# A hybrid attention kernel: the first Toeplitz blocks loaded during the attention, and one half's short lags taken in turns with the last chunks' norm and transform

## The chip, the cores and the metric

The kernel runs on one core of a Trainium2 chip. Its time is the device time of one execution in microseconds (us), taken over three runs; a profile of one further execution shows what each engine did. The engines are TensorE (PE in the profile, PEld for its weight loads), VectorE (DVE), ScalarE (ACT), GpSimd (POOL) and SyncE (SP), which here issues nearly all DMA transfers.

## The reference

Two batches of an image of 128 channels and 64 x 64 places go through a first layer (group norm, 7 x 7 neighbourhood attention, two small dense stages) and a second layer on 4096 tokens of 128 channels. The second layer is what the change touches:

```python
t = _to_tokens(x)
t = t + _L1_attn_ref(_ln_t(t))          # full attention of t with itself, diagonal masked
t = t + _L1_ffn_ref(_ln_t(t), ...)      # "ffn": a spectral unit, below

# in _L1_ffn_ref, for the branch that the gumbel argmax selects (T, T/2, T/4 or T/8 tokens):
U_plus, U_minus = _stu_conv(phi, u, PADDED_SL)        # causal convolution with 16 filters of length sl
out = einsum('btkd,k,kde->bte', U_plus, s, Mpp) + einsum('btkd,k,kde->bte', U_minus, s, Mpm)
for i in range(3):                                    # short lags: tokens t, t-1, t-2
    out = out + einsum('btd,de->bte', shifted(u, i), Mu[i])
```

## The kernel before

**Attention.** `attention(b, fill)` runs for batch 0, then batch 1. The tokens are eight chunks of 512. For each pair of chunks PE computes the products (L896), ACT exponentiates them (L903), PE turns them (L910), DVE copies the turned block and sums its rows (L913), and PE multiplies with the tokens (L924 into `own`, L949 into `other`). When a chunk is complete, `fill(c, part)` is told so; at every other step `fill()` is called without arguments and runs one piece of other work.

**Filler.** `filler(b, steps)` keeps a list `urgent` and the list `steps`. For a complete chunk it adds `after(b, c, part)` to `urgent`, and when four or eight chunks are complete also `short_lags(b, 0)` or `short_lags(b, 1)`. `fill()` runs the next piece of the first generator in `urgent`, or of `steps` if `urgent` is empty. For batch 1, `steps` holds what was left of batch 0 and `filter_matrices`, which loads the filters' matrices through two `st` buffers (L1102) and mixes them on DVE (L1105, L1107, L1118 to L1123). What is left when the attention ends is run then, one generator after another.

**Norm and transform of a chunk.** `after` turns the chunk (L973), divides and adds on DVE (L978), takes the layer norm (statistics L169 and L170 and L159 on DVE, the power on POOL at L160, the result z at L177 on DVE), turns z back (L188, copied to `zc` by ACT at L989), and multiplies it with a segment transform (L1009, L1017), whose results are copied (L1011, L1019) and stored to `us` in HBM (L998).

**Short lags.** `short_lags(b, h)` needs the four chunks of half h of the tokens. In eight pieces it turns the tokens (L188, copied to `xa` by ACT at L1032) and multiplies `zc` with the three matrices `mu` (L1041), which DVE adds to `xa` (L1048).

**Toeplitz products.** After the attention, `pair(q)` loads a block of the filters' transform (`ct`, four DMAs from `gs`, L1256) and a block of the segments' transform (`ut`, one DMA from `us`, L1258) into a pool `conv` of five buffers. `gs` is written during batch 0's attention. `group()` multiplies ct and ut (L1277) into a PSUM tile `pc`, and DVE and ACT copy that to `y` (L1278); `project` multiplies y with the filters' matrices (L1288). Four pairs are loaded ahead.

**What sets the order.** In the Toeplitz loop PE's order is that of the program text; elsewhere in this layer a scheduler orders each engine's instructions, so a DMA may stand earlier in SP's order than in the text. A tile waits for what last used its memory. The pool `conv` lies where `tok`, `cm` and other tiles of the attention lay, and is opened after the attention.

Of the kernel before, what the change touches and what calls it, by code (L numbers as in the profile page):

```python
# [8 lines left out]
F32 = mybir.dt.float32  # L9
# [5 lines left out]
P = 128  # L15
# [6 lines left out]
KF = 16  # L22
# [58 lines left out]
CB, FB, SG = 256, 8, 4  # L81
# [6 lines left out]
LG = 2 * FB  # L88
GROW = 4 * LG * KF
# [3 lines left out]
def kernel(  # L93
# [16 lines left out]
    nc = tc.nc  # L110
# [14 lines left out]
    for c in range(4):  # L125
# [19 lines left out]
        out=flip, in_=flip, compare_op=ALU.not_equal, fill=1.0, base=1 - QT * QT, pattern=[[0, 2], [1, QT * QT]],  # L145
# [39 lines left out]
    def transposed(ps, src):  # L185

        for j in range(src.shape[1]):
            nc.tensor.transpose(ps[:, j * P : (j + 1) * P], src[:, j, :], ident)  # L188
# [30 lines left out]
    with l0a:  # L219
# [34 lines left out]
        def table(ci, h, eng):  # L254
# [16 lines left out]
            out=gavg, in_=gavg, compare_op=ALU.is_ge, fill=0.0, base=0,  # L271
# [3 lines left out]
            out=gavg, in_=gavg, compare_op=ALU.is_ge, fill=0.0, base=3,  # L275
# [524 lines left out]
        for i in range(7):  # L800
# [53 lines left out]
    gs = dram.tile([BINS, 2, SG, GROW], F32, name="gs")  # L854

    with ap_:
# [6 lines left out]
        def bank():  # L863
            return ps_m.tile([P, 512], F32, tag="bank", name="bank")
# [159 lines left out]
        def short_lags(b, h):  # L1024


            for par in range(2):
                n0 = (par * 2 + h) * FB
                for f0 in range(0, FB, 4):
                    pt = bank()  # L1030
                    transposed(pt, tt[b][:, n0 + f0 : n0 + f0 + 4, :])
                    nc.scalar.copy(xa[b][:, (n0 + f0) * P : (n0 + f0 + 4) * P], pt)  # L1032
                    yield
                xv = xa[b][:, n0 * P : (n0 + FB) * P].rearrange("p (f c) -> p f c", f=FB)
                for c0 in range(0, P, 64):
                    py = bank()
                    for lag in range(3):
                        from_par = (par - lag) % 2
                        back = (lag - par + from_par) // 2
                        s0 = 1 + (h * P + c0) * FB - back  # L1040
                        nc.tensor.matmul(  # L1041
                            py, lhsT=mu[:, lag, :], rhs=zc[:, from_par, s0 : s0 + 512], start=(lag == 0), stop=(lag == 2)
                        )
                    pv = py.rearrange("p (c f) -> p f c", f=FB)
                    first = h == 0 and c0 == 0
                    for lo, hi, s in ((0, 32, 0), (32, 64, 1)) if first else ((0, 64, 2 + h),):
                        xs = xv[:, :, c0 + lo : c0 + hi]
                        nc.vector.scalar_tensor_tensor(  # L1048
                            xs, pv[:, :, lo:hi], seg[:, s : s + 1], xs, ALU.mult, ALU.add
                        )  # L1050
                    yield
# [57 lines left out]
        def filter_matrices(mpl, mmi):  # L1109

            for k0 in range(0, KF, 4):
                for dst, src in ((mpl, m_plus), (mmi, m_minus)):
                    mixed(dst[:, k0 : k0 + 4, :], src[:, k0 : k0 + 4])
                    yield

                a, d = (m[:, k0 : k0 + 4, :].rearrange("p k e -> p (k e)") for m in (mpl, mmi))
                s = sp.tile([P, 512], F32, tag="st", name="mdiff")
                nc.vector.tensor_tensor(s, a, d, ALU.subtract)  # L1118
                nc.vector.tensor_tensor(a, a, d, ALU.add)
                for k in range(4):  # L1120
                    ks = slice(k * P, (k + 1) * P)
                    nc.vector.tensor_scalar(a[:, ks], a[:, ks], sg[:, k0 + k : k0 + k + 1], None, ALU.mult)
                    nc.vector.tensor_scalar(d[:, ks], s[:, ks], sg[:, k0 + k : k0 + k + 1], None, ALU.mult)  # L1123
                yield
# [47 lines left out]
            yield from products(1, ((0, b0), (1, b1)))  # L1172
            yield from products(3, ((1, b0),))

        def filler(b, steps):

            urgent, done = [], []

            def fill(c=None, part=None):
                if c is not None:  # L1180
                    done.append(c)
                    urgent.append(after(b, c, part))
                    if len(done) % 4 == 0:
                        urgent.append(short_lags(b, len(done) // 4 - 1))
                    return
                for queue in (urgent, steps):
                    while queue:
                        if next(queue[0], 0) is None:
                            return
                        queue.pop(0)  # L1190

            return fill, urgent
# [25 lines left out]
        mpl = l1.tile([P, KF, P], F32, name="mpl")  # L1218
        mmi = l1.tile([P, KF, P], F32, name="mmi")
        inv = l1.tile([P, 3, CB], F32, name="inv")  # L1220
        steps = [*left, filter_matrices(mpl, mmi)]
        fill, left = filler(1, steps)
        attention(1, fill)
        for gen in (*left, *steps):
            for _ in gen:
                pass

# [8 lines left out]
        nc.vector.tensor_scalar(inv[:, :, lo:hi], inv[:, :, lo:hi], seg[:, s : s + 1], None, ALU.mult)  # L1236
    outf = out.rearrange("b c h w -> b c (h w)")
    with ExitStack() as cv:
        obp = cv.enter_context(tc.tile_pool(name="ob", bufs=1))
        cp = cv.enter_context(tc.tile_pool(name="conv", bufs=5))  # L1240
        ps_c = cv.enter_context(tc.tile_pool(name="ps_c", bufs=6, space=PSUM))
        ps_p = cv.enter_context(tc.tile_pool(name="ps_p", bufs=2, space=PSUM))

        ob = obp.tile([P, 2, NB, FB, BINS, 2], F32, name="ob")

        def pair(q):


            ct = cp.tile([P, 2, 320], F32, tag="ct", name="ct")
            for o in range(2):  # L1250
                for l in range(2):
                    src = bass.AP(
                        gs.tensor, gs.offset + 4 * q * SG * GROW + (2 * o + l) * LG * KF,
                        [[GROW, 4 * SG], [KF, FB], [1, (FB + l) * KF]],
                    )
                    nc.sync.dma_start(out=ct[:, o, l * 144 : l * 144 + (FB + l) * KF], in_=src)  # L1256
            ut = cp.tile([P, NB, 2, P], F32, tag="ut", name="ut")
            nc.sync.dma_start(  # L1258
                out=ut.rearrange("p b s d -> p (b s d)"),
                in_=us[2 * q : 2 * q + 2].rearrange("g i r f b s d -> (g i r f) (b s d)"),  # L1260
            )
            return ct, ut

        def group():


            y = cp.tile([P, 8, KF, 2, 32], F32, tag="y", name="y", bufs=2)
            for q in range(GB // 2):
                ct, ut = ahead.pop(0)
                for par in range(2):  # L1270

                    cv_ = ct[:, :, 0 : 288 + par * 32].rearrange("p o (l c) -> p o l c", l=2)[:, :, :, 0 : FB * KF]
                    for b in range(NB):
                        for f in range(2):
                            fp = slice(f * 64, (f + 1) * 64)
                            pc = ps_c.tile([P, 2, 2, FB * KF], F32, tag="pc", name="pc")
                            nc.tensor.matmul(pc, lhsT=ut[fp, b, par, :], rhs=cv_[fp], start=True, stop=True)  # L1277
                            (nc.scalar.copy if f else nc.vector.tensor_copy)(  # L1278
                                y[:, 4 * f : 4 * f + 4, :, par, b * 2 * FB + q : (b + 1) * 2 * FB : 2],
                                pc.rearrange("p r l (t k) -> p (r l) k t", k=KF),  # L1280
                            )
                if to_load:
                    ahead.append(pair(to_load.pop(0)))
            return y

        def project(g, y, acc, l, k):
# [42 lines left out]

        places = [(b, par, f0) for b in range(NB) for par in range(2) for f0 in range(0, FB, 2)]  # L1330
        to_load = list(range(BINS // 2))
        ahead = [pair(to_load.pop(0)) for _ in range(4)]
        rest = []
        with tc.manual_schedule(engines={mybir.EngineType.PE}):
            y = group()
# [128 lines left out]
```

## Time and profile before

| | |
|---|---|
| median of three runs | 2265.4 us (2261.26 to 2269.05) |
| profiled execution | 2264.99 us, span 2263.3 us, mean granted PE clock 0.988 |
| PE at 1260 to 1280 us, in batch 1's attention | busy 20.00 of 20 us |
| PE from 1307.3 to 1344.0 us, the end of the attention and what is left after it | busy 29.83 of 36.7 us |
| PE from 1344.0 to 1350.1 us | busy 0.01 of 6.1 us |
| PE at 1400 to 1420 us, in the Toeplitz loop | busy 20.00 of 20 us |
| all sixteen DMA engines over the span | 109.76 MB, 48 GB/s |

The busy time of an engine is the time in which it executes; idle time is put down to what ended it. The chain of waits follows the execution back from its last instruction, at each step to what released it. A row of PE's timeline counts records, and a 128 x 512 product in this precision has two.

### The profile page before, as it was taken

Reading aid. Unit: us, or ns where it says so; the run is one execution under the profiler, and the core shown is the slowest. Engines: PE = TensorE matmul, PEld = TensorE weight load, DVE = VectorE, ACT = ScalarE, POOL = GpSimd, SP = SyncE. Lnnn points to the kernel's source line nnn. Section 1 sums busy time; section 2 is a strip of 40 time slices with the busy share of each in tenths; the row PEclk is TensorE's granted clock in tenths of the full one; section 3 lists DMA queues with packets and bytes.
Section 4 is the critical chain, followed back from the end, with each engine's and each line's share of the span. In section 5 each row is a group of like instructions: output and inputs, shape, how many; then the busy total and the mean of one; then the engine's idle time right before and its main releaser. Section 6 shows DMA issues by size and latency. Waiting matters only on the chain.

```text
span 2263.3 us, 31741 instructions
## 1 busy us (share of the span) xinstructions
PE 2187.7 (97%) x11908; PEld 1354.1 (60%) x11908; DVE 940.2 (42%) x3047; ACT 785.3 (35%) x1911; POOL 277.3 (12%) x354
## 2 busy tenths in 40 slices
PE   5899998999999999999999979999999999999998
PEld 3677764544544444544544436777677777767777
DVE  4799985433444347433333333222213222232323
ACT  2789883222333223222222323223323222232322
POOL 3377874200000000000000000000000000000000
PEclk8999998999999999999999989999999999999999
DMA  4222213011100015100000133122222121222101
GB/s 119 63 62 61 61 50 50 0 52 56 38 24 19 6 52 155 33 24 23 1 24 24 39 87 92 42 55 58 44 53 58 39 58 39 57 45 52 41 8 75
DMA packets 180858, 109.76 MB, mean 48 GB/s; under 512 B 32225, under 2 KB 165857, under 8 KB 180194
## 3 DMA queue, kind: packets, MB, share of 16 engines
q1 hardware_dynamic: 177866, 105.47, 17.9%
q10 hardware_dynamic: 2840, 2.27, 0.4%
q8 instruction: 94, 1.54, 0.3%
q14 instruction: 58, 0.48, 0.1%
HBM read 73.09 MB, written 34.60 MB: 48 GB/s over the span
## 4 chain that ended last, share of the span: by engine, by line
PE 87%; DVE 5%; POOL 3%; DMA 1%; ACT 1%; issue 1%; SPq 1%; POOLq 0%; DVEq 0%; ACTq 0%
PE acc L1288 25%; PE pc L1277 13%; PE bank L896 10%; PE own L924 10%; PE other L949 8%; PE bank L910 4%; PE bank L331 2%; PE py L1315 2%; PE bank L188 2%; PE bank L1041 2%; PE bank L1009 2%; PE bank L541 1%; PE bank L1150 1%; PE po L563 1%; PE bank L505 1%
## 5 line engine op out<-in xcount | busy, mean ns | idle before, releaser
L1278 DVE COPY y<-pc 128x512 f32<-128x512 f32 x320 | 221.5, 692 | 358.9 <-PE pc L1277 355.2
L903 ACT ACTIVATE e<-bank 128x512 f32<-128x512 f32 x288 | 171.9, 597 | 563.1 <-PE bank L896 427.2
L896 PE MATMUL bank<-cm 128*128 128x512 f32 x576 | 298.4, 602 | 1.4 <-DVE y L652 1.4
L1277 PE MATMUL pc<-ct,ut 64*128 64x512 f32 x1280 | 287.4, 599 | 6.1 <-issue 6.1
L1288 PE MATMUL acc<-y,mpl 128*128 128x256 f32 x1280 | 292.1, 382 | 0.0
L1288 PE MATMUL acc<-y,mmi 128*128 128x256 f32 x1280 | 288.0, 379 | 0.0
L1288 PEld LDWEIGHTS acc<-y,mpl 128*128 128x128 f32 x1280 | 238.1, 190 | 59.4 <-issue 29.6
L1288 PEld LDWEIGHTS acc<-y,mmi 128*128 128x128 f32 x1280 | 242.6, 190 | 32.6
L1278 ACT COPY y<-pc 128x512 f32<-128x512 f32 x320 | 205.2, 641 | 93.7 <-PE pc L1277 93.7
L949 PE MATMUL other<-e,tok 128*128 128x512 f32 x448 | 228.6, 592 | 0.0
L924 PE MATMUL own<-et,tok 128*128 128x512 f32 x448 | 226.9, 593 | 0.7 <-DVE part L913 0.7
L913 DVE CUSTOM_DVE_ANT_0 et<-bank,one 128x512 f32<-128x512 f32 x224 | 145.7, 688 | 165.0 <-PE bank L910 164.9
L1277 PEld LDWEIGHTS pc<-ct,ut 64*128 64x128 f32 x1280 | 121.8, 188 | 152.8 <-issue 147.7
L1294 ACT COPY ob<-acc 128x256 f32<-128x256 f32 x40 | 24.1, 603 | 430.9 <-PE acc L1288 430.9
L924 PEld LDWEIGHTS own<-et,tok 128*128 128x128 f32 x448 | 84.6, 190 | 108.3 <-issue 72.6
L949 PEld LDWEIGHTS other<-e,tok 128*128 128x128 f32 x448 | 85.0, 190 | 106.6 <-issue 106.2
L896 PEld LDWEIGHTS bank<-cm 128*128 128x128 f32 x576 | 96.4, 193 | 72.4 <-issue 44.5
L1327 DVE TENSOR_TENSOR xa<-py,xa 128x512 f32<-128x512 f32 x32 | 22.2, 692 | 281.4 <-PE py L1315 281.4
L910 PEld LDWEIGHTS bank<-ident,e 128*128 128x128 f32 x896 | 103.3, 141 | 54.1 <-issue 46.2
L160 POOL TENSOR_TENSOR ln_rs<-ln_rs,mhalf 128x4 f32<-128x4 f32 x24 | 24.3, 1012 | 867.0 <-DVE ln_rs L159 867.0
L528 ACT ACTIVATE p<-p,mn 128x196 f32<-128x196 f32 x256 | 114.4, 449 | 22.0 <-DVE mn L518 14.0
L910 PE MATMUL bank<-ident,e 128*128 128x128 f32 x896 | 116.9, 273 | 0.0
(200 smaller groups left out, 2342.8 us busy)
## 6 DMA issues: line engine op xcount, KB each, us to landing
ut<-us SPq DMA_DIRECT2D x80, 256.0 KB
us<-ub SPq DMA_DIRECT2D x64, 256.0 KB
vw<-vd SPq DMA_DIRECT2D x256, 49.0 KB
ct<-gs SPq DMA_DIRECT2D x160, 72.0 KB
ct<-gs SPq DMA_DIRECT2D x160, 64.0 KB
gs<-ub SPq DMA_DIRECT2D x20, 256.0 KB
vd<-v SPq DMA_DIRECT2D x128, 32.0 KB
st<-in_m_plus_dram SPq DMA_DIRECT2D x16, 256.0 KB
```

The costliest lines, as they stand in the source:

```text
L188: nc.tensor.transpose(ps[:, j * P : (j + 1) * P], src[:, j, :], ident)
L331: nc.tensor.matmul(pl, lhsT=wg[:, lo : lo + P], rhs=zT, start=True, stop=True)
L528: nc.scalar.activation(p, p, AF.Exp, bias=t[name + "mn"][:, h : h + 1], scale=-1.0, accum_out=t["den"][:, u, h : h + 1],)
L896: nc.tensor.matmul(ps, lhsT=cm[b][:, n * P : (n + 1) * P], rhs=cm[b][:, chunk(c)], start=True, stop=True)
L903: nc.scalar.activation(e, ps, AF.Exp, bias=0.0, scale=ASCALE, accum_out=part[:, n, c : c + 1])
L910: nc.tensor.transpose(pt[:, k * P : (k + 1) * P], es[k][:, m * P : (m + 1) * P], ident)
L913: nc.vector.tensor_tensor_reduce(et, pt, one, 1.0, 0.0, ALU.mult, ALU.add, part[:, n, a : a + 1])
L924: nc.tensor.matmul(own, lhsT=tok[b][:, n, :], rhs=e, start=first, stop=last)
L949: nc.tensor.matmul(other, lhsT=tok[b][:, 4 * CHUNKS[a] + j, :], rhs=es[j], start=(j == 0), stop=(j == 3))
L1277: nc.tensor.matmul(pc, lhsT=ut[fp, b, par, :], rhs=cv_[fp], start=True, stop=True)
L1278: (nc.scalar.copy if f else nc.vector.tensor_copy)(y[:, 4 * f : 4 * f + 4, :, par, b * 2 * FB + q : (b + 1) * 2 * FB : 2], pc.rearrange("p ...
L1288: nc.tensor.matmul(acc, lhsT=(mmi if l else mpl)[:, k, :], rhs=y[:, 1::2, k, ::-1, :] if l else y[:, 0::2, k, :, :], start=(l == 0 and k = ...
```

## The change

It has four parts.

1. The tile `ct` moves out of `conv` into a pool `blocks` of its own, opened before batch 1's attention. `pair(q)` is split into `blocks(q)`, which loads ct, and `inputs(q)`, which loads ut.
2. A generator `load_blocks`, which loads ct for q = 0 to 3, is added to `steps` of batch 1 after `filter_matrices`. After the attention, only the four ut tiles are loaded ahead.
3. In batch 1, the short lags of the first half are put in a list `kept` instead of `urgent`. When the attention has ended, the rest of `steps` is run, and then what is left of `urgent` (the last chunks' `after` and the second half's short lags) in turns with the kept generator: one piece of the one, one piece of the other.
4. The pool `conv` is opened before the pool of `ob`, where it was opened after it.

```diff
-        def filler(b, steps):
+        def filler(b, steps, kept=None):
...
                     if len(done) % 4 == 0:
-                        urgent.append(short_lags(b, len(done) // 4 - 1))
+                        held = kept if kept is not None and len(done) == 4 else urgent
+                        held.append(short_lags(b, len(done) // 4 - 1))
...
-        steps = [*left, filter_matrices(mpl, mmi)]
-        fill, left = filler(1, steps)
-        attention(1, fill)
-        for gen in (*left, *steps):
-            for _ in gen:
-                pass
...
+        ctp = ctx.enter_context(tc.tile_pool(name="blocks", bufs=5))
+
+        def blocks(q):
+            ct = ctp.tile([P, 2, 320], F32, tag="ct", name="ct")
...
+            return ct
+
+        first_blocks = []
+
+        def load_blocks():
+            for q in range(4):
+                first_blocks.append(blocks(q))
+                yield
+
+        steps = [*left, filter_matrices(mpl, mmi), load_blocks()]
+
+        kept = []
+        fill, left = filler(1, steps, kept)
+        attention(1, fill)
+        for gen in steps:
+            for _ in gen:
+                pass
+        kept = kept.pop()
+        for gen in left:
+            for _ in gen:
+                next(kept, None)
+        for _ in kept:
+            pass
...
-        obp = cv.enter_context(tc.tile_pool(name="ob", bufs=1))
         cp = cv.enter_context(tc.tile_pool(name="conv", bufs=5))
+        obp = cv.enter_context(tc.tile_pool(name="ob", bufs=1))
...
-        def pair(q):
-            ct = cp.tile([P, 2, 320], F32, tag="ct", name="ct")
...
+        def inputs(q):
             ut = cp.tile([P, NB, 2, P], F32, tag="ut", name="ut")
...
-            return ct, ut
+            return ut
...
-                    ahead.append(pair(to_load.pop(0)))
+                    q_ = to_load.pop(0)
+                    ahead.append((blocks(q_), inputs(q_)))
...
-        ahead = [pair(to_load.pop(0)) for _ in range(4)]
+        ahead = [(ct, inputs(to_load.pop(0))) for ct in first_blocks]
```

Line numbers in the text up to here are those of the kernel before.

More of the change, by code (lines that the diff above doesn't have):

```diff
@@ L1220 @@
         inv = l1.tile([P, 3, CB], F32, name="inv")
-        steps = [*left, filter_matrices(mpl, mmi)]
-        fill, left = filler(1, steps)
-        attention(1, fill)
-        for gen in (*left, *steps):
-            for _ in gen:
-                pass
-    tb_ = nc.inline_tensor(t_out, "t_out").ap().rearrange("(a p) c -> p a c", p=P)
-    nc.sync.dma_start(out=inv, in_=tb_)
-    for s, (lo, hi) in enumerate(((0, 32), (32, 64), (64, 128), (128, 256))):
-        nc.vector.tensor_scalar(inv[:, :, lo:hi], inv[:, :, lo:hi], seg[:, s : s + 1], None, ALU.mult)
-    outf = out.rearrange("b c h w -> b c (h w)")
-    with ExitStack() as cv:
-        obp = cv.enter_context(tc.tile_pool(name="ob", bufs=1))
[L1240 to L1244, printed above, removed]
-        def pair(q):
-            ct = cp.tile([P, 2, 320], F32, tag="ct", name="ct")
+        ctp = ctx.enter_context(tc.tile_pool(name="blocks", bufs=5))
+        def blocks(q):
+            ct = ctp.tile([P, 2, 320], F32, tag="ct", name="ct")
             for o in range(2):
@@ L1256, in pair @@
                     nc.sync.dma_start(out=ct[:, o, l * 144 : l * 144 + (FB + l) * KF], in_=src)
+            return ct
[17 more added lines that the diff above has]
+            pass
+    tb_ = nc.inline_tensor(t_out, "t_out").ap().rearrange("(a p) c -> p a c", p=P)
+    nc.sync.dma_start(out=inv, in_=tb_)
+    for s, (lo, hi) in enumerate(((0, 32), (32, 64), (64, 128), (128, 256))):
+        nc.vector.tensor_scalar(inv[:, :, lo:hi], inv[:, :, lo:hi], seg[:, s : s + 1], None, ALU.mult)
+    outf = out.rearrange("b c h w -> b c (h w)")
+    with ExitStack() as cv:
+        cp = cv.enter_context(tc.tile_pool(name="conv", bufs=5))
+        obp = cv.enter_context(tc.tile_pool(name="ob", bufs=1))
+        ps_c = cv.enter_context(tc.tile_pool(name="ps_c", bufs=6, space=PSUM))
+        ps_p = cv.enter_context(tc.tile_pool(name="ps_p", bufs=2, space=PSUM))
+        ob = obp.tile([P, 2, NB, FB, BINS, 2], F32, name="ob")
+        def inputs(q):
             ut = cp.tile([P, NB, 2, P], F32, tag="ut", name="ut")
```

## The prediction

> **What bounds the kernel now.** I read the page's busy table and slices first. TensorE (PE) is busy for 97% of the span, so whatever shortens PE's own path shortens the kernel; the only slice in mid-kernel that falls below 9 is slice 24, at about 1301 to 1358 us.
>
> ```profile
> PE 2187.7 (97%) x11908; PEld 1354.1 (60%) x11908; DVE 940.2 (42%) x3047; ACT 785.3 (35%) x1911; POOL 277.3 (12%) x354
> PE   5899998999999999999999979999999999999998
> ```
>
> That slice is the passage from the attention to the Toeplitz products. Second view: PE's timeline there, where a bracket is idle time before the row and what ended it.
>
> ```profile
> 1308.67 1.98 PE L924 MATMUL own<-et,tok 128*128 128x512 f32 x4 [0.35 <-DVE part L913]
> 1311.44 1.13 PE L924 MATMUL own<-e,tok 128*128 128x512 f32 x2 [0.78 <-DVE xa L928]
> ...
> 1317.18 1.00 PE L188 MATMUL bank<-ident,z 128*128 128x128 f32 x4 [1.60 <-DVE z L177]
> ...
> 1325.78 1.24 PE L188 MATMUL bank<-ident,z 128*128 128x128 f32 x4 [4.09 <-DVE z L177]
> ...
> 1350.09 15.32 PE L1277 MATMUL pc<-ct,ut 64*128 64x512 f32 x60 [6.14 <-issue]
> ```
>
> The reader sees five waits, 12.96 us together; the two large ones are 4.09 (the last chunk's norm, DVE and POOL in series) and 6.14 (before the first product). Third view: the chain of waits, which shows what the 6.14 is made of and how fast PE ran around it.
>
> ```profile
> 1318.19 1.92 PE bank L1009 x8
> ...
> 1327.03 3.71 PE bank L1009 x8
> ...
> 1338.80 5.17 PE bank L1041 x12
> ...
> 1344.02 0.56 SPq L1256
> ...
> 1345.91 2.97 DMA ct<-gs
> 1348.88 1.21 issue
> ```
>
> SP issues the first ct load only when the last L1041 matmul has ended at 1343.97. The product also needs ut, SP's fifth issue (1346.55 for 0.59), so its landing fits the "issue" of 1.21. The two L1009 rows are the same eight matmuls, 1.92 and 3.71 us; the windows of 2 us say why (the third number from the right is PE's granted clock, after the busy times and counts of the engines):
>
> ```profile
> 1322.00:1324.00 2.00, 0.00 (x0) 0.00 (x0) 1.99 (x12) 0.59 (x1) 0.00 (x0) 0.95 0.94 284
> 1328.00:1330.00 2.00, 2.00 (x8) 0.66 (x4) 0.69 (x1) 0.73 (x2) 0.00 (x0) 0.50 0.00 0
> 1352.00:1354.00 2.00, 2.00 (x8) 1.03 (x6) 0.81 (x2) 0.72 (x2) 0.00 (x0) 0.50 0.29 72
> ```
>
> **What the Trainium skill says.** "TensorE: Matmul & The Clock Gate", What's actually happening: PE drops to half clock after an idle window of about 3.4 us and needs a busy one to recover, in windows that run free. The trace agrees: 0.50 after 4.09 and after 6.14 us. The trace adds that from 850 to 852 us the clock is 0.50 after a wait of only 1.60 us with thin work before it, while at 1317 the same wait costs nothing. "DMA: Bandwidth & Descriptors", Latency and other measured facts: a transfer has about 2 us of fixed cost; here the ct load shows 2.97 us after issue. "Perfetto Trace Analysis", Optimizing Tensor Performance, Matmuls: groups that rotate through PSUM banks let ACT and DVE empty one during the next; the tail has six banks, and before the change no row of it waits long for one.
>
> **The change part by part**, against the profiled span of 2263.3 us (that execution took 2264.99, the median is 2265.4, so a saving is taken from the median unchanged).
>
> *Short lags of the first half moved.* One half is two times (8 transposes, 0.87, and 6 matmuls, 5.16): 12.06 us of PE. Before, the first half stood in the attention between 1206.85 and 1239.7, where PE is at 20.00 of 20. Without it the attention is as full (1260 to 1280, with none of it, has 20.00 too), so it ends 12.06 us earlier and the same 12.06 come back in the tail: net nothing. The DVE and ACT work with it (6 L1048, 4 L1032) goes along.
>
> *What it fills.* In the built program's order, PE now has after the last chunk's transposes (L973) two groups of three L1041 matmuls, 5.16 us, ahead of the z transposes. The chain from L973 to z took 4.09 us. Two short L1048 now stand in DVE's order after L159, while POOL works for 1.04, and one stands behind z. The wait goes: -4.09. Waits 0.35, 0.78 and 1.60 stand ahead of the first moved piece and remain. PE then doesn't go cold there: L1009 3.71 to 1.92 and L188 1.24 to 1.00, -2.03.
>
> *Loads.* All of q = 0 to 4, 20 ct issues, now stand in SP's order where the filter matrices load (from 846.56 us). Of the first products' needs only ut stays behind. In the built order its first issue waits for the us stores and for the last L188 transpose, no longer for L1041. Six L1041 follow that transpose: 5.16 us. Issue 0.59 plus about 3 us of landing is 3.6, so it is there 1.5 us ahead of PE. What the first product then waits for is its bank, whose last reader is the last L1048 on DVE: 0.75 us after the last matmul plus handover, 0.85. Gap 6.14 to 0.85: -5.29. The first 64 product rows took 16.18 us, 32 later ones 7.07; kept warm they cost 14.14: -2.04. The second buffer of y and the later uts come behind by 0.6 us an issue, and eight products are 3.5 us, so they hide.
>
> *What it costs at 846 to 926.* Twenty ct issues at 0.61 are 12.2 us of SP, and 20 x 68 KB are 1.36 MB, at the 200 GB/s that busy windows there show 6.8 us of DMA. SP's rows:
>
> ```profile
> 846.56 0.36 SPq L1234 DMA_DIRECT2D inv<-t_out  x1
> 849.18 1.16 SPq L1102 DMA_DIRECT2D st<-in_m_plus_dram  x2
> ...
> 853.91 5.36 SPq L1102 DMA_DIRECT2D st<-in_m_minus_dram  x4
> ...
> 862.74 0.37 SPq L1102 DMA_DIRECT2D st<-in_m_plus_dram  x1
> ```
>
> Behind a late st stands DVE's L1107, behind that DVE's et (L913) and z, and PE waits for those. But SP itself waits there: each st waits for DVE to free one of two buffers. Laying the 20 issues into the order by hand, four fill 846.56 to 849.0 and nearly all others gaps such as 855.1 to 857.3, so no st is issued over a microsecond late; landing may be. DVE's order there also puts the chunk's tt ahead of four of the six L1122/L1123 it stood behind (4 x 0.2 earlier) and L1105 (0.49) after z. PE's wait at 869.70 is 1.89 now. I bound the stretch by -1.9 (wait gone) and +3 (a microsecond on three st), and take +0.8.
>
> *New small waits.* Banks emptied in turn by ACT (L989 takes 1.09, L1032 0.54): 0 to 1.5, taken 0.5. A cold clock after the 1.60 wait, as at 850 (L1009 x4 1.86 against 0.96, ten L896 rows 5.48 against 4.3): 0 to 2.1, taken half, 1.0.
>
> The new pool order (conv ahead of ob) moves addresses only, and the Toeplitz loop keeps its order on PE and its loads: 0. Sum: -4.09 - 2.03 - 5.29 - 2.04 + 0.8 + 0.5 + 1.0 = -11.15. The forecast is 2265.4 - 11.15 = 2254.3 us.
>
> **Rivals.**
> *ut takes ct's place.* The first product waits for ut instead. For it: ut waits for every us store and a transpose in the tail. Against: 1.5 us of room, and DMA is idle (0.00) from 1336 to 1344. If five uts together land 3 us late, the gap is about 2.5 to 4 and the clock may drop: 2265.4 - 7.5 = 2258.
> *The turns don't fill.* PE, in order, sits behind a short-lag piece whose bank or xa copy isn't ready, and the last chunk's chain gets longer by DVE's and ACT's extra rows. For it: ACT is in order and L989 precedes L1032. Against: ACT and DVE were busy 7.74 and 15.19 of the 36.7 us from 1307.3. Keeping half of 4.09 and half of 2.03, and 2 us of new waits: 2265.4 - 11.15 + 5 = 2259.3.
> *Slower.* The ct loads at 846 hold the filter loads, and through DVE's order the attention. Price: 12.2 of SP and 6.8 of DMA, 19 us if PE paid it all, less what is saved (11.95 without this term): 2272.5. It decides once PE's idle time in 846 to 926 grows from 3.48 to over 15.4 us. Against: the gaps counted above, and DVE is busy 57 of 80.
> That the change doesn't do what it says (ct still late) has the built order against it; I give it no share of its own.
>
> **How the numbers follow.** Forecast 0.70, ut 0.10, unfilled turns 0.13, slower 0.07. The forecast's own terms span -13.45 - 1.9 to -13.45 + 6.6, mostly 2251 to 2258. With the before runs at 2261.26 to 2269.05, a new median is itself uncertain by some 3 us; the range 2248.5 to 2261 leaves out most of the slower case and the far ends. A measurement of this kernel tells about 0.3%, 6.8 us, from no change: faster means below 2258.6. That is 0.66 of the forecast's 0.70, 0.07 of ut's, 0.05 of the turns' : 0.78. Slower by as much is most of the last case, 0.05; the rest, 0.17, is within.
>
> **What would show it.** In the new profile: no idle over 1 us ahead of the last z transposes; L1009 at 1.9 there; the first product within about 1 us of the last L1041, released by DVE; the first 64 products near 14.1 us; clock 1.00 throughout; PE idle in 846 to 926 within 2 us of 3.5. It is wrong if the product is still released by a DMA or SP, if the clock still shows 0.50 at the passage, or if the attention of the second batch ends less than 10 us earlier.

## The result, and the profile after

| | before | after |
|---|---|---|
| median (six executions of each, side by side) | 2264.35 us (2261.26 to 2269.05) | 2254.17 us (2252.96 to 2258.94) |
| ratio of after to before, 95% interval | | 0.9955 (0.994 to 0.997) |
| span of the profiled execution | 2263.3 us | 2251.2 us |

The change is 10.2 us faster, with 6.8 to 13.6 in the interval; the forecast was 2254.3, a saving of 11.15. Measured once more beside other kernels the ratio was 0.9957 (0.994 to 0.9974). The code below L1218 moved in the listing: after's L1234 loads ct (before L1256), L1280 loads ut (L1258), L1299 is the first product (L1277), L1311 the projection (L1288), L1265 loads `inv` (L1234). The listings of the experiments are shifted by some lines again; the names of the tiles tell which row is meant.

The page of after, its busy table and the slices of PE:

```profile
PE 2183.3 (97%) x11908; PEld 1352.2 (60%) x11908; DVE 939.8 (42%) x3047; ACT 783.8 (35%) x1911; POOL 276.8 (12%) x354
PE   5899998999999999999999999999999999999998
```

The count of PE's instructions is the same; slice 24, a 7 before, is now a 9. PE's timeline of after at the passage from the attention to the products (start, length, engine, line, what, and in brackets the idle time before the row and what ended it):

```profile
1297.95 1.98 PE L924 MATMUL own<-et,tok 128*128 128x512 f32 x4 [0.35 <-DVE part L913]
1300.71 1.12 PE L924 MATMUL own<-e,tok 128*128 128x512 f32 x2 [0.78 <-DVE xa L928]
...
1306.45 1.00 PE L188 MATMUL bank<-ident,z 128*128 128x128 f32 x4 [1.60 <-DVE z L177]
...
1311.83 5.32 PE L1041 MATMUL bank<-zc,mu 128*128 128x512 f32 x12
1316.98 0.60 PE L188 MATMUL bank<-ident,z 128*128 128x128 f32 x4
...
1340.21 14.00 PE L1299 MATMUL pc<-ct,ut 64*128 64x512 f32 x64 [0.89 <-issue]
```

The three small waits 0.35, 0.78 and 1.60 are still there. The 4.09 ahead of the last z transposes has no bracket any more: six L1041 (twelve records) stand in it. The 6.14 ahead of the first product is 0.89, and the first 64 product records take 14.00 us, where they took 16.18. The chain of waits of after in the same place (start, length, what) and the windows of 2 us (busy time of each engine, then PE's granted clock, the DMA share and GB/s) show the clock:

```profile
1318.02 1.06 PE bank L1009 x4
...
1319.66 1.06 PE bank L1009 x4
...
1334.17 5.15 PE bank L1041 x12
1339.32 0.89 issue
1340.21 14.00 PE pc L1299 x64
```

```profile
1318.00:1320.00 2.00, 2.00 (x11) 0.96 (x12) 0.69 (x1) 1.97 (x4) 0.00 (x0) 1.00 0.00 0
...
1342.00:1344.00 2.00, 2.00 (x12) 1.11 (x10) 1.50 (x4) 1.38 (x4) 0.00 (x0) 1.00 0.03 8
```

The eight L1009 records that took 3.71 us at a clock of 0.50 take twice 1.06 at 1.00. No DMA stands ahead of the product; SP's rows of after say when ut was issued:

```profile
1325.15 1.24 SPq L998 DMA_DIRECT2D us<-ub  x2
1334.24 2.24 SPq L1280 DMA_DIRECT2D ut<-us  x5
```

The first ut goes out at 1334.24, right after the last transpose, and the product starts 5.97 us later. In experiment 4, where ut is late, a product starts 3.14 us after this issue, so here ut has landed under the last six L1041, and what the product still waits for is on DVE (further below).

To see where the 12.1 us between the two spans lie, I cut each at three marks: A, the start of the z transposes near 848 us that wait 1.59 or 1.60; B, the L924 near 1300 with the wait of 0.35; C, the first product. D is the first projection. 12.06 us of short lags move from the stretch A to B into the stretch B to C; the table takes them out of the comparison.

| stretch | before | after | difference without the moved lags |
|---|---|---|---|
| start to A (first layer and what leads up to the filter loads) | 848.12 | 847.65 | -0.47 |
| A to B (filter loads, attention of batch 1) | 460.55 | 450.30 | +1.81 |
| B to C (the passage) | 41.42 | 42.26 | -11.22 |
| C to D (first products) | 16.1 | 13.9 | -2.2 |
| D to end | 897.1 | 897.1 | 0.0 |

So the passage and the first products gave 13.4 us and the stretch with the early loads took 1.8 back in this execution.

### The profile page after: what moved, and what is told of

Its sections match the earlier page's. It is cut to its first block, busy times and chain, and to the rows that moved or that the text cites. A ratio compares the mean times of both kernels' runs of the same rounds, so it can differ in the third digit from the quotient of the medians.

```text
span 2251.2 us, 31746 instructions
## 1 busy us (share of the span) xinstructions
PE 2183.3 (97%) x11908; PEld 1352.2 (60%) x11908; DVE 939.8 (42%) x3047; ACT 783.8 (35%) x1911; POOL 276.8 (12%) x354
## 4 chain that ended last, share of the span: by engine, by line
PE 85%; DVE 6%; POOL 3%; DMA 3%; ACT 1%; issue 1%; SPq 1%; DVEq 0%; ACTq 0%; POOLq 0%
PE acc L1311 25%; PE pc L1299 13%; PE bank L896 9%; PE own L924 9%; PE other L949 8%; PE bank L910 4%; PE py L1338 2%; PE bank L331 2%; PE bank L188 2%; PE bank L541 1%; PE bank L1041 1%; PE bank L1009 1%; PE bank L1150 1%; DMA st<-in_m_minus_dram 1%; PE po L563 1%
## 5 line engine op out<-in xcount | busy, mean ns | idle before, releaser
L1311 PE MATMUL acc<-y,mpl 128*128 128x256 f32 x1280 | 292.1, 382 | 0.0
L1311 PE MATMUL acc<-y,mmi 128*128 128x256 f32 x1280 | 288.0, 379 | 0.0
L1299 PE MATMUL pc<-ct,ut 64*128 64x512 f32 x1280 | 285.2, 595 | 0.9 <-issue 0.9
L1311 PEld LDWEIGHTS acc<-y,mpl 128*128 128x128 f32 x1280 | 238.1, 190 | 59.4 <-issue 29.6
L1311 PEld LDWEIGHTS acc<-y,mmi 128*128 128x128 f32 x1280 | 242.6, 190 | 32.7
L924 PE MATMUL own<-et,tok 128*128 128x512 f32 x448 | 227.2, 594 | 1.9 <-DVE part L913 1.9
L913 DVE CUSTOM_DVE_ANT_0 et<-bank,one 128x512 f32<-128x512 f32 x224 | 145.7, 688 | 166.7 <-PE bank L910 166.6
L1299 PEld LDWEIGHTS pc<-ct,ut 64*128 64x128 f32 x1280 | 121.5, 187 | 145.8 <-issue 140.6
L924 PEld LDWEIGHTS own<-et,tok 128*128 128x128 f32 x448 | 84.3, 190 | 110.4 <-issue 72.4
L528 ACT ACTIVATE p<-p,mn 128x196 f32<-128x196 f32 x256 | 114.4, 449 | 21.6 <-DVE mn L518 13.9
```

The lines of the kernel that those rows point to most:

```text
L528: nc.scalar.activation(p, p, AF.Exp, bias=t[name + "mn"][:, h : h + 1], scale=-1.0, accum_out=t["den"][:, u, h : h + 1],)
L913: nc.vector.tensor_tensor_reduce(et, pt, one, 1.0, 0.0, ALU.mult, ALU.add, part[:, n, a : a + 1])
L924: nc.tensor.matmul(own, lhsT=tok[b][:, n, :], rhs=e, start=first, stop=last)
L1311: nc.tensor.matmul(acc, lhsT=(mmi if l else mpl)[:, k, :], rhs=y[:, 1::2, k, ::-1, :] if l else y[:, 0::2, k, :, :], start=(l == 0 and k = ...
```

## The experiments

Each kernel is the change or the kernel before with one edit. The time saved is the ratio's distance from 1 times the median of before measured beside it.

**1. The early loads without the moved lags.**

```diff
-        fill, left = filler(1, steps, kept)
+        fill, left = filler(1, steps)
```

and what is left after the attention runs one generator after another, as before.

> The change without its turns: blocks loaded early and the new pool order stay, the first half's short lags run in the attention as before. Theory (the savings are separate and add up): the gap ahead of the first product is 0.9 us instead of 6.14 and its first 64 rows take 14.0 instead of 16.18, the filter loads cost 1.2 to 1.5, so 5.8 to 6.3 us faster than before; the wait of 4.09 us ahead of the last z transposes and the half clock after it are still there. Rival (the two halves of the change need one another, since the moved lags are what gives ut its time): gap of 3 us or more, 0 to 3 us faster. Rival (the whole gain is the loads'): 10 us faster.

2260.55 against 2266.46 us, ratio 0.9973 (0.9962 to 0.9983): 6.1 us, as expected. The stretch of the filter loads costs 4.05 us in its profile, where 1.2 to 1.5 was expected (table under 11). PE's timeline:

```profile
1332.59 1.25 PE L188 MATMUL bank<-ident,z 128*128 128x128 f32 x4 [4.08 <-DVE z L177]
1333.76 3.79 PE L1009 MATMUL bank<-z,tr 64*128 64x512 f32 x8
...
1351.78 13.57 PE L1296 MATMUL pc<-ct,ut 64*128 64x512 f32 x62 [0.89 <-issue]
```

The gap before the product is closed by the early loads, the pool of their own and the pool order, without the turns; the 4.08 and the half clock behind it stay.

**2. The turns without the early loads.** The kernel before, with `kept` and the turns of the change, and the pools and loads as they were.

> The kernel before with only the turns: the first half's short lags kept and taken in turns after the attention, loads and pools as before. Theory: the 4.09 us wait goes and L1009 there takes 1.1 per pair of products, 5.9 to 6.1 us faster than before; the gap of 6.1 us ahead of the first product and its slow first rows stay, and the filter loads' stretch is as before. Rival (the turns only move the wait to bank and xa copies in the tail): 0 to 3 us faster. Rival (the whole gain is the turns'): 10 us faster.

2259.8 us, ratio 0.9967 (0.9955 to 0.998): 7.5 us, with 4.5 to 10.2 in the interval, which holds the 5.9 to 6.1 expected. PE's timeline has the old gap and the slow first products:

```profile
1344.77 16.79 PE L1285 MATMUL pc<-ct,ut 64*128 64x512 f32 x64 [6.05 <-issue]
```

and no wait ahead of the last z transposes. Each half of the change thus does its own half of the work at the passage, and they don't need each other. By the times the two come to 13.6 us, more than the change's 10.2, but each is uncertain by some 3. By the profiles they add up: from B to C, moved lags taken out, 1 saves 3.47 and 2 saves 6.04; 1 also lost 1.65 there to a slow clock behind the wait of 1.60 that neither 2 nor the change had. With that put back they make 11.16, and the change saves 11.22.

**3. The lags moved, but not taken in turns.**

```diff
         for gen in left:
             for _ in gen:
-                next(kept, None)
+                pass
         for _ in kept:
             pass
```

> The change, but the kept short lags run after everything that is left and not in turns with it. Theory (moving them is worth nothing by itself, since PE is full in the attention): as the kernel with the loads alone, 5.8 to 6.3 us faster than before, and the attention ends about 12 us earlier with 12 us more behind it. Rival (the lags cost more outside the attention, where copies of banks are not covered): 1 to 3 us slower than the kernel with the loads alone.

2262.82 us, ratio 0.9981 (0.9972 to 0.999): 4.3 us. Its profile has the wait of the unchanged order:

```profile
1319.47 1.24 PE L188 MATMUL bank<-ident,z 128*128 128x128 f32 x4 [4.09 <-DVE z L177]
```

Its median is 2.3 us above experiment 1's, which is what the rival named, but the intervals overlap. From B to C its profile saves 5.6 us with the moved lags taken out, no less than experiment 1's, so the passage shows no cost of moving them. Nor is there a gain: it is the turns that make the moved lags useful, and the change itself saves about 6 us more than this kernel.

**4. The pools in their old order.**

```diff
-        cp = cv.enter_context(tc.tile_pool(name="conv", bufs=5))
         obp = cv.enter_context(tc.tile_pool(name="ob", bufs=1))
+        cp = cv.enter_context(tc.tile_pool(name="conv", bufs=5))
```

> The change with one line put back: the pool of ob opened ahead of conv, as before. The prediction held this order for worth nothing. Theory of now (it decides which memory ut gets, and so what ut waits for): ut waits for the last L1041 again; gap of 3.6 to 4.0 us instead of 0.9, 2.8 us slower than the change if the clock stays at 1.00, up to 4.9 if it falls, so 5.3 to 7.4 us faster than before. Rival (as the prediction had it): gap 0.9, the same as the change, 10 us faster than before.

2261.11 us, ratio 0.9967 (0.9954 to 0.9979): 7.5 us, some 2.7 less than the change, with intervals that overlap; it is the profile that shows the loss. SP's row and the chain of waits of this kernel:

```profile
1343.56 2.24 SPq L1280 DMA_DIRECT2D ut<-us  x5
```

```profile
1338.37 5.17 PE bank L1041 x12
1343.54 0.02 issue
1343.57 0.76 DVE xa L1048
1344.33 2.37 issue
1346.70 13.52 PE pc L1299 x53
```

ut is issued at 1343.56, when the last L1041 has ended at 1343.54, and the product waits 3.17 us; its first 64 records take 15.70. In the profile that is 2.3 us at the gap and 1.7 at the products. In the built program ut's first load waits for the last L1041 here, and in the change for the last L188, six of PE's matmuls earlier. Opened first, `conv` spans the tiles `tt`, `tok` and `cm` of batch 1, of which the short lags' transposes read `tt`; opened second, it reaches `mu` and `zc`, which L1041 reads. ut's own bytes lie on `cm` in this kernel, which no L1041 reads: the first load waits for all that the pool spans, and not, as said above, for what last used the tile's memory alone. The one reordered line is therefore a part of the saving, and not a change of addresses only.

**5. The early loads made twice.** Each of the 20 ct loads is issued two times in a row, with the same data.

```diff
-                    nc.sync.dma_start(out=ct[:, o, l * 144 : l * 144 + (FB + l) * KF], in_=src)
+                    for _ in range(2 if q < 5 else 1):
+                        nc.sync.dma_start(out=ct[:, o, l * 144 : l * 144 + (FB + l) * KF], in_=src)
```

> The change with the first five blocks' loads issued twice each (40 ct issues instead of 20 in the stretch of the filter loads, the same data). It asks what an issue costs there. Theory (a late st passes through DVE's order to PE, and only what no gap of SP takes is late): PE idle from 846 to 926 us grows from 4.4 to 6 to 9 us, 2 to 5 us slower than the change. Rival slower case of the prediction (PE pays each issue, 0.61 us): 12 us slower than the change. Rival (SP's gaps take all, the waits at 902 and 921 us have another cause): no change.

2256.4 against 2264.74 us, ratio 0.996 (0.9945 to 0.9974): about 1 us less saved than by the change, inside what the intervals leave open. The expected 2 to 5 us did not show. In SP's order many of the added issues stand behind the four `m_minus` loads that turn out to matter (eight ct issues in a row at 866.53, the last of those four at 860.12), so doubling was a poor measure of the cost.

**6. The early loads made late in the attention.** The five ct tiles are first touched by POOL with a value of the fourth complete chunk, and `load_blocks` joins `steps` when the fifth chunk is complete.

```diff
+                    if kept is not None and len(done) == 5:
+                        steps.append(load_blocks())
...
+            if q < 5:
+                n0 = 4 * CHUNKS[3]
+                for o in range(2):
+                    for l in range(2):
+                        nc.gpsimd.tensor_copy(ct[:, o, l * 144 : l * 144 + 1], tt[1][:, n0, 0:1])
```

> The change with the first five blocks loaded later in the attention: POOL first writes one column of each part of the tile from the fourth complete chunk, so that the loads wait for that chunk, some 300 us after the filter loads. Theory (the early loads' cost is the filter loads' delay): PE idle from 846 to 926 us is back at 3.3 to 3.6, no wait for DVE at 902 us, 1 to 1.5 us faster than the change; the passage stays as it is. Rival (the loads delay whatever they are put among, here the us stores): the wait appears at 1150 to 1250 us instead, same time as the change.

2253.75 us, ratio 0.9945 (0.993 to 0.996): 12.5 us. The 20 issues stand at 1193.47 to 1208.6 us, where no filter load is; the gap before the product is 1.03. The stretch A to B costs 0.72 us over before, and the change's wait of 0.95 for L913 at 902.59 is gone with the loads. PE's idle time from 846 to 930 us is 4.22 us, not the 3.3 to 3.6 expected. The intervals of this kernel and of the change overlap, so that it is faster than the change is likely, not shown.

**7. The kernel before, with PE kept busy in the gap.** Five additional products of `ident` with part of `xa`, whose result nobody reads, stand ahead of the first product.

```diff
+        n1 = 3 * FB
+        dum = ps_o.tile([P, 512], F32, tag="other", name="dum")
+        for _ in range(5):
+            nc.tensor.matmul(dum, lhsT=ident, rhs=xa[1][:, (n1 + 4) * P : (n1 + 8) * P], start=True, stop=True)
```

> The kernel before with five extra 128x512 products on PE in the gap of 6.14 us ahead of the first Toeplitz product (their result is not used). It asks for the clock alone: the gap stays. Theory: with PE busy there the clock stays at 1.00, the first 64 product rows take 14.1 us instead of 16.18, 2.0 us faster than before. Rival (the first rows were slow because ct and ut were still landing): 16 us, no change.

2263.68 us, ratio 0.9993 (0.9986 to 0.9999): 1.6 us (0.2 to 3.2), as expected. In its timeline the useful work starts hardly earlier (11.25 us after the last L1041 row begins, 11.46 before), but faster:

```profile
1341.51 4.53 PE L1230 MATMUL dum<-xa,ident 128*128 128x512 f32 x10 [0.94 <-DVE xa L1048]
1346.51 14.38 PE L1281 MATMUL pc<-ct,ut 64*128 64x512 f32 x64 [0.47 <-PE dum L1230]
```

This prices the cold clock behind the gap by itself: 64 records take 14.38 in place of 16.18. That ct and ut were still landing, the rival, is not what slowed them.

**8. Later loads, and the turns begun in the last pair of chunks.** As 6, and from the seventh complete chunk on every other `fill()` runs a kept piece.

```diff
+                if kept and len(done) >= 7:
+                    turn[0] = not turn[0]
+                    if turn[0] and next(kept[0], 0) is None:
+                        return
```

> The kernel with the later loads, and the kept short lags begun in the attention's last pair, one piece at every second step, so that the waits of 0.78 and 1.60 us ahead of the change's first moved piece have work beside them. Theory (what is idle there is the chain's latency, and any ready work fills it): 1.5 to 2.4 us faster than the kernel with the later loads, 2.5 to 4 us faster than the change. Rival (fewer pieces are left for the last chunk's chain, whose wait comes back): 1 us faster or none.

2250.77 us, ratio 0.9936 (0.992 to 0.9953): 14.5 us, the lowest time of all. But the profile doesn't credit the earlier turns with it. From A to C it takes 491.60 us and kernel 6 takes 491.62; its span is 3.0 us shorter (2249.1 against 2252.1), and those 3.0 lie ahead of A (846.90 against 849.86), which the edit can't reach. Whether a part of the lower median is the edit's own stays open. Its timeline has lost 0.35 and 1.60 and got this:

```profile
1306.04 0.33 PE L188 MATMUL bank<-ident,z 128*128 128x128 f32 x1 [2.61 <-DVE z L177]
```

By the profile the rival of its expectation held: the wait came back in another place.

**9. Later loads, and only two kept pieces taken early.** As 6, and two pieces of transposes (0.87 us of PE) run when six chunks are complete, so that L1041 groups come up sooner in the turns.

> The blocks' loads wait for a late chunk as in the run with loads later; and two of the kept pieces (eight transposes of a half, bank and copy each) are taken in the attention before its last pair, so that in the last chunks' tail other pieces of the half, some L1041 groups, come between the transposes and z. My theory (only PE work placed into a wait saves time, its place alone doesn't): the 1.60 ahead of the third-last z transposes is filled at least partly, the 4.09 one stays filled, and the passage from the z transposes at 848 to the first product is 0.5 to 1.6 us shorter than the 491.6 of the two kernels with late loads; time 13 to 14.5 us below before. Rival (as in the run with turns begun in the last pair): a wait comes back elsewhere, and the passage is 491.6 again, time about 12.5 below before.

2257.1 against 2265.58 us, ratio 0.9963 (0.995 to 0.9976): 8.4 us, some 4 less than kernel 6; A to C is 497.09 in place of 491.6. Both the theory and its rival had expected better. PE's timeline shows why:

```profile
1309.67 2.84 PE L1041 MATMUL bank<-zc,mu 128*128 128x512 f32 x6
...
1313.45 2.84 PE L1041 MATMUL bank<-zc,mu 128*128 128x512 f32 x6
1316.13 0.60 PE L973 MATMUL bank<-ident,xa 128*128 128x128 f32 x4
...
1321.12 0.45 PE L188 MATMUL bank<-ident,z 128*128 128x128 f32 x1 [3.52 <-DVE z L177]
```

The two L1041 groups now stand ahead of L973. L973 is the head of the last chunk's norm: it starts 9.31 us after the z transposes at 1306.82, in the change 4.94 us after those at 1306.45. The groups delay the chain that they should hide, and nothing is left to stand in its wait. What is filled in counts only behind the head of the chain.

**10. The early loads issued by ACT.**

```diff
-                    nc.sync.dma_start(out=ct[:, o, l * 144 : l * 144 + (FB + l) * KF], in_=src)
+                    (nc.scalar if q < 5 else nc.sync).dma_start(out=ct[:, o, l * 144 : l * 144 + (FB + l) * KF], in_=src)
```

> The change with the 20 ct issues of the first five blocks in ACT's order in place of SP's; the transfers are the same and about as early. Theory 1 (SP's order is what costs: st loads are issued behind ct issues): the stretch from the z transposes at 848 to the attention's end costs 0 to 0.7 us over before, as in the kernels without early loads, unless ACT's 20 issues cost PE something; time 11.5 to 12.5 below before. Theory 2 (the transfers' traffic delays the st loads): the stretch still costs 1.8 or more and the time is as the change's, about 10 below before. Third: the issues hold ACT, which empties PE's banks there; then over 2.5 in the stretch, and new PE waits on ACT.

2254.5 us, ratio 0.9956 (0.9941 to 0.9971): as the change. In its profile A to B costs 6.77 us over before. SP's row of this kernel, then DVE's rows of this kernel and of the kernel before, for the first and the fourth of the four `m_minus` loads:

```profile
850.92 6.89 SPq L1102 DMA_DIRECT2D st<-in_m_minus_dram  x4
```

```profile
855.53 0.49 DVE L1105 TENSOR_SCALAR mmi<-st,wt 128x512 f32<-128x512 f32 x1 [3.33 <-DMA st<-in_m_minus_dram]
...
863.88 0.75 DVE L1107 SCALAR_TENSOR_TENSOR mmi<-st,wt,mmi 128x512 f32<-128x512 f32 x1 [3.78 <-DMA st<-in_m_minus_dram]
```

```profile
856.80 0.48 DVE L1105 TENSOR_SCALAR mmi<-st,wt 128x512 f32<-128x512 f32 x1 [0.99 <-DMA st<-in_m_minus_dram]
...
861.97 0.75 DVE L1107 SCALAR_TENSOR_TENSOR mmi<-st,wt,mmi 128x512 f32<-128x512 f32 x1 [0.92 <-DMA st<-in_m_minus_dram]
```

The first is issued 5.74 us after A here (850.92 - 845.18) and was issued 5.79 after A before (853.91 - 848.12). DVE gets it 4.61 us after the issue here, 2.89 before; it gets the fourth 6.43 us after its issue (857.45), 3.06 before (858.91). SP's order is that of before, and the loads are late all the same: in this profile it is the transfers that hold them. The sixteen DMA engines are busy for 0.95 of the 6 us behind A here, 0.72 in the change and 0.67 before.

With the ct loads on SP the same shows, but not in every load. The first `m_minus` load takes 2.89 to 3.31 us in the six kernels without early loads (before, 2, 6 to 9) and 3.06 to 3.67 in the six profiles with them on SP; the fourth takes 3.02 to 3.36 and 3.10 to 5.68. SP's own order adds a little: the first filter load goes out 1.65 to 1.67 us after A with them, 1.04 to 1.06 without. This fits what the Trainium skill says in "DMA: Bandwidth & Descriptors", Issuing engines are not separate DMA queues: whatever engine starts them, the transfers run on the same sixteen DMA engines and interleave.

Two things blur the size. ACT, too, was held at 859.46, 6.62 us in its last two issues, which the third expectation had foreseen. And ACT's issues stand closer than SP's did: 17 of the 20 go out ahead of the fourth `m_minus` load, in the change 10. The direction is shown; the 6.77 is not what the traffic of the change costs.

**11. The change once more**, on the chip of 9 and 10.

> The change itself once more, on the same chip as the two runs beside it: 2254 us, 10 us below before (ratio 0.9955), the first product 0.9 us after the last L1041. In its profile the stretch from the z transposes at 848 to the attention's end either costs 1.8 us over before again (then the single profiled execution stands for the kernel), or anything up to the 5 us that other kernels with early loads showed (then this stretch varies between executions, and the single profile can't size the cost of the early loads).

2255.63 us, ratio 0.9957 (0.994 to 0.9974). The passage is the same to the hundredth, 42.26 from B to C with a gap of 0.89. The stretch A to B isn't: it costs 5.68 us over before, where the first profile of the same kernel had 1.81; that one was the fastest of its six executions, this one the slowest of its four. PE's and DVE's timelines:

```profile
871.88 1.25 PE L188 MATMUL bank<-ident,z 128*128 128x128 f32 x4 [5.55 <-DVE z L177]
...
907.59 1.12 PE L924 MATMUL own<-et,tok 128*128 128x512 f32 x2 [1.33 <-DVE part L913]
```

```profile
857.57 0.49 DVE L1105 TENSOR_SCALAR mmi<-st,wt 128x512 f32<-128x512 f32 x1 [2.24 <-DMA st<-in_m_minus_dram]
...
864.94 0.75 DVE L1107 SCALAR_TENSOR_TENSOR mmi<-st,wt,mmi 128x512 f32<-128x512 f32 x1 [3.16 <-DMA st<-in_m_minus_dram]
```

DVE waits for st, z stands behind that in DVE's order, and PE waits 5.55 us for z at 871.88 (1.89 before). A single profile can't size this cost; all of them together can bound it:

| kernel | ct loads among the filter loads | DVE idle for st, 844 to 880 us | A to B over before, moved lags taken out |
|---|---|---|---|
| before | no | 5.1 | 0 |
| 2, 6, 7, 9 | no | 5.5, 4.8, 5.1, 4.6 | 0.74, 0.72, 0.59, 1.26 |
| the change, twice | yes | 6.3, 8.6 | 1.81, 5.68 |
| 1, 3, 4, 5 | yes | 6.7, 8.2, 8.3, 6.2 | 4.05, 5.18, 5.37, 3.19 |
| 10 | yes, by ACT | 10.5 | 6.77 |

The two groups don't overlap in either column (kernel 8 has no mark B; its first column is 5.1). The mean of the seven with early loads is 4.6 us, of the four without 0.8: by these profiles the early loads cost some 4 us there, between 1 and 6 in one execution.

The granted clock in the few us behind A sorts them once more. It falls to 0.50 in three profiles, before, the change's first and 9, and there the stretch costs 0, 1.81 and 1.26. It stays at 1.00 in all others: 0.59 to 0.74 without the early loads, 3.19 to 5.68 with them on SP. Like compared with like, they cost 0.6 to 1.8 us where the clock fell and 2.5 to 5.1 where it didn't, so the 1.81 of the change's first profile belongs to the rarer kind of execution.

By the times it is less: kernel 6, which takes them out of this stretch, saves 2.3 us more than the change, within intervals that overlap. I take 2 to 4 as an estimate from both.

## Why the prediction was right, and where it wasn't

The time was right, 2254.3 forecast and 2254.17 measured. That they agree so closely is chance: the kernel before came to 2264.35 beside it and not to 2265.4, and the saving was 10.2 in place of 11.15. Step by step:

- *The bound and the place.* Right: PE's path, and on it the passage. D to end is unchanged to a tenth. (Slice 24 is not the only one below 9 in mid-kernel: the seventh, 340 to 396 us, shows an 8 before and after, where the change doesn't reach.)
- *Lags moved, net nothing.* Right: the attention's end (B), counted from A, comes earlier by 10.25, which is 12.06 less the stretch's 1.81, and experiment 3 finds no gain in the move itself. In the change's second profile B comes only 6.38 earlier, under the 10 that the prediction named as a sign of being wrong. The moved lags are the same there; what differs is the stretch, with 5.68.
- *The 4.09 and the cold clock behind it.* Right, 4.09 to no wait and 3.71 to 2.12 for the eight L1009. A short L1048 does stand in the chain, as DVE's timeline of after shows, and costs little (the last row is for the next point):

```profile
1314.31 0.17 DVE L159 TENSOR_SCALAR ln_rs<-ln_mv 128x4 f32<-128x4 f32 x1
1314.67 0.88 DVE L1048 SCALAR_TENSOR_TENSOR xa<-bank,seg,xa 128x256 f32<-128x256 f32 x2 [0.19 <-PE bank L1041]
1315.67 1.12 DVE L177 TENSOR_SCALAR z<-tt,ln_mv,ln_rs 128x128 f32<-128x128 f32 x4
...
1339.36 0.75 DVE L1048 SCALAR_TENSOR_TENSOR xa<-bank,seg,xa 128x512 f32<-128x512 f32 x1 [1.76 <-PE bank L1041]
```

- *The gap before the first product and the products behind it.* Right in size: 6.14 to 0.89 (0.85 said). The last L1048 ends at 1340.11 (1339.36 + 0.75) and the product starts at 1340.21; in the built program it waits for this L1048, besides its loads and an ACT copy (L1032) long done, so it is that bank. And 14.00 for 64 records (14.14 said). The named wrong step is beside it: "the new pool order (conv ahead of ob) moves addresses only ... 0". The gap of 0.85 was read from the built order, in which the pool order was already at work; taken back alone it costs 2.7 us of time and 4.0 in the profile (experiment 4). The sum was right because the saving was booked under the loads; the reason given for it was incomplete.
- *The stretch from 846 to 926.* This term was mis-sized: +0.8, with bounds of -1.9 and +3. Six of the seven executions profiled with early loads lie above +3, one of the change's own two among them. The way was named rightly (a late st, DVE's order, z, PE). The working laid out SP's issues and found no st over a microsecond late, which holds for the first `m_minus` load: 5.78 us after A, 5.79 before. It then took the landing for nearly as quick as before, and the landing is what gave way: 3.67 us in place of 2.89 for that load in the change's first profile, 5.60 in place of 3.06 for the fourth in the second. PE's idle time in 846 to 930 was 4.63 in the first profile of the change and 8.63 in the second, so the test set in the prediction ("within 2 us of 3.5") failed in the second.
- *New small waits and a cold clock after the 1.60.* 1.5 was allowed; in both profiles of the change some 0.05 came: the stretch from B to D gave 13.4 of the 13.45 gross. The worry about the clock was sound: behind the same wait of 1.59 or 1.60 the eight L1009 records took 1.99 us in nine profiles and 2.98, 3.63 and 3.68 in experiments 1, 5 and 10.

So the forecast's total stands on 13.4 saved at the passage, as worked out, and on two errors of opposite sign: some 2 to 4 us for the early loads in place of 0.8, and nothing for the new waits in place of 1.5. That they partly cancel was luck. With the mean of the change's two profiles, 3.75, the sum is -9.65; measured were -10.2 and, as a ratio of 0.9957, -9.7.

Of the rivals, *ut takes ct's place* is what the kernel does with the pools in their old order: a gap of 3.17 us, within the 2.5 to 4 that it named; *the turns don't fill* is what experiments 8 and 9 show of other turns; *slower* had its mechanism right and its price far too high: the stretch cost 2 to 7 us, and PE's idle time there was never over 8.63 us, where 15.4 would have decided.

## What to carry to other kernels

Work that fills a wait must stand behind the instruction that starts the chain and ahead of the one that ends it: the same pieces one place earlier lengthened the chain and cost 4 us. A load moved out of a gap isn't free where it lands: look for transfers in flight there and for who stands behind them in an engine's order, and look for a stretch without them, as the loads at 1193 us had. When a load waits for memory, the order in which pools are opened decides whose last reader it waits for, so read each tile's releaser in the built order before calling a reordered line neutral.

## What was not expected of the hardware

- The same instructions after the same wait of 1.60 us run slower, the granted clock at 0.50 for some 3 us, in some executions and at full clock in others: in three of the twelve profiles that have that wait ahead of the eight L1009 records, and near 848 us in three of thirteen, other ones. The Trainium skill, "TensorE: Matmul & The Clock Gate", What's actually happening, says that the window in which activity is counted runs free, so that the number of slow matmuls varies from run to run; it puts the idle window at about 3.4 us, while here a wait of 1.60 us, with other waits of 0.35 and 0.78 in the 9 us before it, was enough.
- The time ahead of A, which no edit touches, ranged from 844.75 to 849.86 us over the profiles: a spread of 5 us, half the change's saving, that comes from outside the part under study. Comparing stretches between landmarks, not spans, is what kept experiment 8 from being misread.
- What the runs can't settle: why the early loads cost 1.81 in one execution of the change and 5.68 in the other. The clock at 848 to 852 differs (half in the first, full in the second, so that PE comes to the z transposes earlier and waits longer there), and all other profiles sort the same way. But the loads for the filters land later in the second as well (the fourth `m_minus` 5.60 us after its issue, 3.10 in the first), and no run sets the clock by itself.
